# A block-matching convolution kernel on one core: row slots outermost, aggregation and cosine transform copied by ScalarE, transform on 32x32 tiles

## The chip, the cores and the metric

The kernel runs on one core of a Trainium2 chip. The metric is the time of one execution on the device, in microseconds (us); lower is better. Before the change the median of three runs is 6639.3 us (6633.16 to 6649.49).

The core has five engines that run side by side, each through its own list of instructions in order: PE (TensorE, matrix multiplication), DVE (VectorE), ACT (ScalarE), POOL (GpSimd) and SP (SyncE). SP and POOL mostly issue DMAs here. Instructions wait for each other through semaphores.

## The reference

The input x is [8, 32, 128, 128] in float32. Two layers are computed; each normalises its input, computes a branch and adds it to its input. Cut to what matters:

```python
def _L0_conv_ref(x, dct_w, w1, w2, w3, w4, w5, w6, inv_dct_w, agg_w):
    B, C, K, H, W = (8, 32, 8, 128, 128)
    CK = C * K
    # for each pixel: the K of 25 offsets with the lowest 3x3 patch distance,
    # then the K shifted copies of x: [B, C*K, H, W], channel c*K + k
    xb = _patch_match_stack(x)
    dct = _conv(xb, dct_w, groups=C)
    h = jax.nn.relu(_conv(_conv(xb, w1), w2, groups=CK, pad=1))
    h = jax.nn.relu(_conv(_conv(h, w3), w4, groups=CK, pad=1))
    wiener = jax.nn.sigmoid(_conv(_conv(h, w5), w6, groups=CK, pad=1))
    filt = _conv(wiener * dct, inv_dct_w, groups=C)
    return _conv(filt, agg_w)

# --- layer 0 ---
x = x + _L0_conv_ref(_gn(x), ...)
# --- layer 1: one 5x5 kernel on every channel ---
x = x + _L1_conv_ref(_gn(x), L1_conv_kernel, 1, 2)
```

w1, w3, w5 are 256x256 pointwise weights; w2, w4, w6 are 3x3 depthwise weights. The cosine transform (dct) mixes only the 8 copies of one channel: 32 blocks of 8x8.

## The kernel before

**Steps and turns.** An image has 128 rows. The main loop (from L1054) makes 17 steps of 8 rows per image, 136 in all; the last step of an image (n == NS) only finishes rows. Each step has four turns, `i` = 3, 2, 1, 0. In turns 3, 2 and 1 the step does one of the three convolution pairs (pointwise, then depthwise, then its function) for an earlier and earlier stage of the pipeline: conv `i` works on the rows of step s - (i - 1). Turn 0 is the end: cosine transform, product with the result of conv 3, and, a turn later, the aggregation.

**A convolution pair.** The 256 channels are in two halves. The first half goes through `pointwise_t` (PE, L694), a copy by ACT into the buffer `t` (L701), and `depthwise_t`, which does the 3x3 taps as matmuls on PE (pw, L750) and evacuates them by ACT (L763). The second half goes through `pointwise_v` (pv, L670), an ACT copy into `tv` (L678), and `depthwise_v`: first tap on ACT (L721), eight taps on DVE (L724), function on ACT (L728). `t` holds, for each of 128 partitions (4 rows of a group x 32 channels), 4 channel blocks q x 4 row slots x 128 columns. The slots hold the rows that the next matmuls need; SP fills slots from others by DMA, from one half of the partitions to the other (L648, L706, L708).

**Gathering.** Every turn also gathers pixels of a later step: `gather_load` (POOL DMAs, `ib` and `xt`), `gather_select` (ACT, L616 and L617, two 128x1024 operations, twice a turn), `gather_pixels` (PE pg, L631, and an ACT copy into `xb`, L638). After the last copy of a step, POOL stores `xb` to DRAM as `xbd` (L640), one DMA of 1 MB; the layout in DRAM has partition and half as its first two axes.

**The end of a step.** `final_load` (POOL) reads the rows of x (`xr`, L780) and of the gathered copies (`xf`, L790, eight DMAs) for the step before; there is one `xf` buffer. `final_dct` multiplies with the block-diagonal `ldct`, on tiles of 64 rows by 64 columns: 8 matmuls into four `pc` buffers (L809), and DVE multiplies conv 3's result by each of them, straight from PSUM (L817). `final_add` is a generator whose parts run at calls of `next(later)`: the aggregation matmuls `pa` (L830), then, after a `yield`, DVE adds `pa` to `xr` (L838), takes statistics (L839), and POOL stores `xr` as `x1d` (L843).

**PSUM.** `ps_x` has five buffers that go round, for pv, p, pg, pc, pa and others; `ps_dw` has two for pw.

**Order.** PE, DVE and ACT execute in the order in which the code is written (`manual_schedule`); POOL's and SP's order is chosen by the scheduler. POOL's DMAs go through eight semaphores in turn, so an issue waits for the DMA that used the same one before. Work for later images (`prep`, `squares`, `costs`, `places`) and layer 1 of finished ones (`layer1`, `middle`) lies in four queues: "D" for DVE work with a cost in us, which `tick` hands out at a set amount per turn, 40% of a step's in turn 0 and 20% in each other; "A", "P" and "Q" for what follows on ACT and PE.

The turn's order is, shortened (L1065 to L1110):

```python
pointwise_v(i, ...); new_v, new_t = depthwise_v(...), depthwise_t(...)
next(later, None)           # pa on PE, in turn 3
run("P")
if live and not i: final_dct(...)
run("Q"); gather_select(u + 1, (0,)); gather_load(u + 3); tick(b, i)
next(later, None)           # sum on DVE, in turn 3
next(new_v, None)           # eight taps on DVE
pointwise_t(i, ...)
next(kept, None); gather_pixels(u)
next(dt, None)              # pw matmuls of the turn before
run("A"); next(dv, None)    # function of the turn before
gather_select(u + 1, (1,)); next(dt, None)
```

**Set-up.** `mixes` loads `dct_w` into `dq` by 32 small DMAs on SP (L308) and forms `ldct` from it on DVE (L311, L318).

Of the kernel before, what the change touches and what calls it, by code (L numbers as in the profile page):

```python
# [16 lines left out]
P = 128  # L17
C, K, H, W = 32, 8, 128, 128
CK = C * K
# [25 lines left out]
def bm3d_conv_preact(  # L45
# [61 lines left out]
    ldct = const.tile([P, 2, 64], F32, name="ldct")  # L107
# [192 lines left out]
    def mixes():  # L300

        dq = work.tile([P, 2, K], F32, name="dq", tag="dq", bufs=1)
        src = dct_w.rearrange("(m h c i) k a b -> m h k c (i a b)", m=2, h=2, i=K)
        for k in range(K):
            for m in range(2):
                for h in range(2):
                    p = 64 * h + 32 * (k % 2) + 8 * (k // 2)
                    nc.sync.dma_start(dq[p : p + 8, m], src[m, (h + m + 1) % 2, k])  # L308
        m8 = work.tile([P, 8], F32, name="m8", tag="m16", bufs=1)
        yield "D", 1.0, 10  # L310
        nc.vector.tensor_reduce(  # L311
            m8,
            cst[:, C_M32 : C_M32 + C].rearrange("p (a c) -> p c a", c=8),
# [3 lines left out]
        for m in range(2):  # L317
            nc.vector.tensor_tensor(  # L318
                ldct[:, m].rearrange("p (c i) -> p c i", i=K),
                m8.unsqueeze(2).to_broadcast([P, 8, K]),  # L320
                dq[:, m].unsqueeze(1).to_broadcast([P, 8, K]),
                ALU.mult,
            )
# [296 lines left out]
    def gather_pixels(b, s4, f):  # L620
# [18 lines left out]
        if h == 1 and f == 1:  # L639
            nc.gpsimd.dma_start(xbd[b][:, :, R * n : R * (n + 1)], xb)  # L640
# [3 lines left out]
    def rows_before_t(i, b, n):  # L644

        t = tb[i - 1]
        if n < NS:
            nc.sync.dma_start(t[0:64, :, 0], t[64:P, :, 3])  # L648
        else:
            nc.gpsimd.memset(t[0:64, :, 0], 0.0)  # L650
# [29 lines left out]
    def pointwise_t(i, b, n, lhsT, src):  # L680
# [3 lines left out]
        if n == NS and i == 1:  # L684
            nc.gpsimd.memset(t[:, :, 2], 0.0)
        else:
            for q in range(2):
                ps = ps_x.tile([P, 2, 2, W], F32, name=f"p{i}_{b}_{n}_{q}", tag="x")
                for e in range(2):
# [12 lines left out]
                    t[: C * nr, 2 * q : 2 * q + 2, 2 : 2 + nb], ps[: C * nr, :, :nb]  # L702
                )
            for r in range(i - 1) if n == 0 else range(i - 1, 4) if n == NS else ():
                nc.gpsimd.memset(t[C * r : C * (r + 1), :, 2], 0.0)
        nc.sync.dma_start(t[64:P, :, 0:nb], t[0:64, :, 2 : 2 + nb])  # L706
        if nb == 2:
            nc.sync.dma_start(t[0:64, :, 1], t[64:P, :, 2])  # L708
# [23 lines left out]
    def depthwise_t(i, b, n):  # L732
        t = tb[i - 1].rearrange("p q (h k) w -> p q h k w", k=2)
# [35 lines left out]
    def final_load(b, n):  # L769
# [15 lines left out]
        src = xbd[b].rearrange("(j m h c) g y x -> g m h j c y x", j=4, m=2, h=2)  # L785
        for m in range(2):
            for h in range(2):
                for g in range(2):
                    p = 64 * h + C * g
                    nc.gpsimd.dma_start(  # L790
                        xf[p : p + C, m, j0:j1], src[g, m, (h + m + 1) % 2, :, :, ya:yz]
                    )
        return xr, xf, j0, j1

    def final_dct(b, n, acc, xf, j0, j1):

        for r0 in range(0, R, 4):
            a, z = max(r0, j0), min(r0 + 4, j1)
            if a >= z:
                continue  # L800


            pc = [
                ps_x.tile([P, 4, W], F32, name=f"pc_{b}_{n}_{m}_{r0}", tag="x") for m in range(2)
            ]
            for h in range(2):
                for m in range(2):
                    o = 64 * ((h + m + 1) % 2)
                    nc.tensor.matmul(  # L809
                        pc[m][o : o + 64, : z - a],  # L810
                        ldct[64 * h : 64 * h + 64, m],
                        xf[64 * h : 64 * h + 64, m, a:z],
                        start=True,
                        stop=True,
                    )
            for m in range(2):
# [360 lines left out]
```

## Time and profile before

| | |
|---|---|
| median of three runs | 6639.3 us (6633.16 to 6649.49) |
| profiled execution, its own time | 6645.45 us |
| its span | 6643.7 us |
| mean granted PE clock over the span | 0.978 |
| L724, eight taps on DVE, busy | 4032.3 us |
| L750, depthwise matmuls on PE, busy | 2124.6 us |
| L616 and L617, selects on ACT, busy | 1172.1 and 1085.7 us |
| L790, issues of the xf loads on POOL, busy | 651.9 us |
| chain of waits, by engine | PE 43%, DVE 29%, DMA 9%, ACT 8%, POOL 6% |

The span is the time that the profiler saw between the first and the last instruction; the execution's time holds a little more. Busy times of one engine add up to its share of the span; those of different engines overlap. A row of a group reads: line, engine, operation, output <- inputs, shape, count | busy us, mean ns of one | us idle just before, and what ended that idle time. PE's matmuls are pipelined: several run at once, so the mean of one is longer than the busy time divided by the count.

### The profile page before, as it was taken

What the parts mean: (1) busy time and instruction counts of PE and PEld (TensorE: products, weight loads), DVE (VectorE), ACT (ScalarE), POOL (GpSimd) and SP (SyncE); (2) the same over time, 40 slices, a digit from 0 to 9 for tenths busy, and PEclk for the clock granted to TensorE, in tenths of its full rate; (3) what the DMA queues carried; (4) which work ended last, traced back from release to release, by engine and by line L of the source; (5) the groups of instructions that cost most, each with busy time, mean ns of one, the idle gap of its engine ahead of it and who ended that gap; (6) DMA issues with size and microseconds to landing.
All of it is one profiled execution on the core that took longest, in us unless ns stands there. A gap on an engine that the chain in (4) does not pass through costs nothing.

```text
span 6643.7 us, 234197 instructions
## 1 busy us (share of the span) xinstructions
PE 6238.3 (94%) x102306; PEld 3236.5 (49%) x102306; DVE 5862.9 (88%) x8828; ACT 5054.4 (76%) x6698; POOL 3079.3 (46%) x5015
## 2 busy tenths in 40 slices
PE   5898899999999999999999999999999999999997
PEld 1444455544555545544555544554445544454553
DVE  7889988999889998898989998899888999887786
ACT  5787778777787777877778877887769777687772
POOL 8354346444464343643446444464435543344334
PEclk8899999999999999999999999999999999999998
DMA  4555555656555564655646656465555655556553
GB/s 85 126 138 130 131 131 130 148 134 140 131 143 136 130 147 118 149 134 133 144 121 147 147 126 149 120 154 136 130 137 132 148 136 130 125 141 145 137 133 82
DMA packets 770751, 886.20 MB, mean 133 GB/s; under 512 B 248880, under 2 KB 614000, under 8 KB 769728
## 3 DMA queue, kind: packets, MB, share of 16 engines
q0 software_dynamic: 383648, 611.87, 36.9%
q1 hardware_dynamic: 383568, 258.11, 17.6%
q8 instruction: 805, 13.19, 0.9%
q10 hardware_dynamic: 2512, 1.25, 0.1%
q14 instruction: 218, 1.79, 0.1%
HBM read 420.60 MB, written 216.49 MB: 96 GB/s over the span
## 4 chain that ended last, share of the span: by engine, by line
PE 43%; DVE 29%; DMA 9%; ACT 8%; POOL 6%; issue 4%; SPq 0%; ACTq 0%; DVEq 0%; POOLq 0%
DVE acc L724 20%; PE pw L750 14%; PE pv L670 11%; PE p L694 9%; PE pg L631 3%; DMA t<-t 3%; POOL xtd L424 2%; DVE df L444 2%; DVE idx L537 2%; PE pc L809 2%; ACT sel L616 2%; ACT df L452 2%; DMA xf<-xbd 2%; DVE acc L817 1%; PE p L923 1%
## 5 line engine op out<-in xcount | busy, mean ns | idle before, releaser
L724 DVE SCALAR_TENSOR_TENSOR acc<-tv,dwv,acc 128x1024 f32<-128x1024 f32 (+3 forms) x3264 | 4032.3, 1237 | 240.8 <-ACT acc L721 136.8
L750 PE MATMUL pw<-t,dwd 96*32 96x254 f32 (+7 forms) x31680 | 2124.6, 420 | 51.0 <-DMA t<-t 38.4
L750 PEld LDWEIGHTS pw<-t,dwd 96*32 96x32 f32 (+1 forms) x31680 | 1088.4, 110 | 874.5 <-issue 411.2
L616 ACT ACTIVATE sel<-ib,nplace 128x1024 f32<-128x1024 uint8 x1024 | 1172.1, 1145 | 37.4 <-DMA ib<-idxd 37.4
L617 ACT ACTIVATE sel<-sel 128x1024 f32<-128x1024 f32 x1024 | 1085.7, 1060 | 32.5
L694 PE MATMUL p<-acc,lw 128*32 128x256 f32 x16768 | 1002.9, 383 | 24.7 <-ACT tv L678 23.3
L670 PE MATMUL pv<-acc,lw 128*32 128x512 f32 x8448 | 956.2, 590 | 48.7 <-DVE acc L817 43.4
L602 POOL DMA_DIRECT2D ib<-idxd x512 | 292.5, 571 | 1241.8 <-ACT sel L616 1176.2
L790 POOL DMA_DIRECT2D xf<-xbd x1088 | 651.9, 631 | 316.1 <-PE pc L809 180.1
L694 PEld LDWEIGHTS p<-acc,lw 128*32 128x32 f32 x16768 | 579.2, 111 | 437.1 <-issue 79.4
L452 ACT ACTIVATE df<-df 128x786 f32<-128x786 f32 (+2 forms) x576 | 468.6, 861 | 340.5 <-DVE df L444 337.8
L631 PE MATMUL pg<-sel,xt 120*32 120x88 f32 (+1 forms) x24576 | 616.1, 244 | 63.6 <-ACT sel L617 50.7
L631 PEld LDWEIGHTS pg<-sel,xt 120*32 120x32 f32 x24576 | 556.8, 110 | 235.0 <-ACT sel L617 70.1
L678 ACT COPY tv<-pv 128x512 f32<-128x512 f32 (+2 forms) x784 | 437.1, 579 | 305.0 <-PE pv L670 293.0
L444 DVE TENSOR_TENSOR df<-xn 128x786 f32<-128x786 f32 (+2 forms) x576 | 531.6, 973 | 81.2 <-PE pd L459 80.2
L728 ACT ACTIVATE acc<-acc 128x1024 f32<-128x1024 f32 (+3 forms) x408 | 417.3, 1023 | 241.6 <-DVE acc L724 241.3
L763 ACT ACTIVATE acc<-pw 128x512 f32<-128x512 f32 (+2 forms) x808 | 438.5, 573 | 182.7 <-PE pw L750 182.0
L670 PEld LDWEIGHTS pv<-acc,lw 128*32 128x32 f32 x8448 | 286.0, 111 | 534.1 <-issue 428.7
L701 ACT COPY t<-p 128x512 f32<-128x512 f32 x800 | 424.4, 571 | 118.0 <-PE p L694 118.0
L721 ACT ACTIVATE acc<-tv,dwv 128x1024 f32<-128x1024 f32 (+3 forms) x408 | 454.9, 1115 | 33.9 <-PE pa L830 20.6
L670 PE MATMUL pv<-xb,lw 128*32 128x512 f32 x4096 | 473.5, 596 | 0.0
L694 PE MATMUL p<-xb,lw 128*32 128x256 f32 x8192 | 468.5, 379 | 1.0 <-DVE xy L935 0.9
(155 smaller groups left out, 5932.9 us busy)
## 6 DMA issues: line engine op xcount, KB each, us to landing
ib<-idxd POOLq DMA_DIRECT2D x512, 256.0 KB, 4.1
xbd<-xb POOLq DMA_DIRECT2D x128, 1024.0 KB, 5.9
xf<-xbd POOLq DMA_DIRECT2D x960, 128.0 KB, 7.1
t<-t SPq DMA_DIRECT2D x792, 128.0 KB
t<-t SPq DMA_DIRECT2D x384, 256.0 KB
tv<-tv SPq DMA_DIRECT2D x384, 130.0 KB
xt<-xtd POOLq DMA_DIRECT2D x240, 180.0 KB, 3.7
xtd<-xl POOLq DMA_DIRECT2D x192, 96.0 KB, 3.5
```

The source lines that it names most:

```text
L444: nc.vector.tensor_sub(df[:, :, ca:cz], xn[:, r0 : r0 + SR, ca:cz], xn[:, r0 + dy : r0 + dy + SR, ca + dx : cz + dx],)
L452: nc.scalar.activation(df[:, :, ca:cz], df[:, :, ca:cz], AF.Square)
L616: nc.scalar.activation(sel, ib, AF.Square, bias=nplace)
L617: nc.scalar.activation(sel, sel, AF.Relu, scale=-1.0, bias=1.0)
L631: nc.tensor.matmul(pg[C * j : C * (j + 1), :, :, xa:xz], xt[: 8 * QW, f * (NT // 2) + t], sels[j // 2][: 8 * QW, j % 2 * 2 : j % 2 * 2 + 2 ...
L670: nc.tensor.matmul(ps[C * j : C * (j + 1), :hr], lhsT[:, g, P + C * j : P + C * (j + 1)], src(g)[:, h : h + hr], start=g == 0, stop=g == 1,)
L694: nc.tensor.matmul(ps[C * r : C * (r + 1), e, :nb], lhsT[:, g, s], rows[:, r : r + 4 * nb - 3 : 4], start=g == 0, stop=g == 1,)
L721: nc.scalar.activation(acc, rows, AF.Copy, scale=tap)
L724: nc.vector.scalar_tensor_tensor(acc, rows, tap, acc, op0=ALU.mult, op1=ALU.add)
L750: nc.tensor.matmul(pt[u][C * j : C * (j + 1), ka:kz, :nb, xa:xz], dwd[0:hi, i - 1, u, j, dx + 1], t[0:hi, j, ka:kz, :nb, xa + dx : xz + dx ...
L763: nc.scalar.activation(rows[:, u : u + 2 * nh[u] - 1 : 2, :nb], pt[u][:, : nh[u], :nb], funcs[i - 1])
L790: nc.gpsimd.dma_start(xf[p : p + C, m, j0:j1], src[g, m, (h + m + 1) % 2, :, :, ya:yz])
```

## The change

- `ldct` and `dq` are laid out for 32x32 blocks, four per half; the loads of `dct_w` become 64.
- `xbd` holds the 256 channels in natural order. `xb` is stored twice a step, after each group of four rows, by four DMAs each.
- In `t` the row slot becomes the outermost of the free axes: slot, block, column, for block, slot, column. All users of `t` follow.
- `final_load` becomes a generator: the `xr` loads come first, where they were; the `xf` loads (one or two DMAs for each of four pieces of half m and four rows, the channels turned by 32 x s) are issued two pieces at the end of the next turn 3 and two at the end of turn 2.
- `final_dct` does four matmuls on 32x32 tiles for each piece s, from row block q to column block (q + s) mod 4. ACT copies each result over its input in `xf`; DVE then multiplies conv 3's result by `xf`, two instructions for four.
- `final_add` copies `pa` by ACT into a tile `xs`, and adds it one part later; the loop has one more `next(later)` at the end of a turn.

```diff
-    ldct = const.tile([P, 2, 64], F32, name="ldct")
+    ldct = const.tile([P, 4, C], F32, name="ldct")
...
-        for k in range(K):
-            for m in range(2):
-                for h in range(2):
-                    p = 64 * h + 32 * (k % 2) + 8 * (k // 2)
-                    nc.sync.dma_start(dq[p : p + 8, m], src[m, (h + m + 1) % 2, k])
+        for s in range(4):
+            for q in range(4):
+                for c in range(4):
+                    p = C * q + K * c
+                    nc.sync.dma_start(dq[p : p + K, s], src[s // 2, (q + s) % 4, c])
...
-        if h == 1 and f == 1:
-            nc.gpsimd.dma_start(xbd[b][:, :, R * n : R * (n + 1)], xb)
+        if f == 1:
+            for j in range(4):
+                nc.gpsimd.dma_start(
+                    xbd[b].rearrange("(c j g) y x -> j c g y x", j=4, g=2)[
+                        j, :, :, 4 * s4 : 4 * s4 + 4
+                    ],
+                    xb[C * j : C * (j + 1), :, 4 * h : 4 * h + 4],
+                )
...
-            nc.sync.dma_start(t[0:64, :, 0], t[64:P, :, 3])
+            nc.sync.dma_start(t[0:64, 0], t[64:P, 3])
...
                 nc.scalar.copy(
-                    t[: C * nr, 2 * q : 2 * q + 2, 2 : 2 + nb], ps[: C * nr, :, :nb]
+                    t[: C * nr, 2 : 2 + nb, 2 * q : 2 * q + 2].rearrange("p b e w -> p e b w"),
+                    ps[: C * nr, :, :nb],
                 )
...
-        nc.sync.dma_start(t[64:P, :, 0:nb], t[0:64, :, 2 : 2 + nb])
+        nc.sync.dma_start(t[64:P, 0:nb], t[0:64, 2 : 2 + nb])
         if nb == 2:
-            nc.sync.dma_start(t[0:64, :, 1], t[64:P, :, 2])
+            nc.sync.dma_start(t[0:64, 1], t[64:P, 2])
...
-        t = tb[i - 1].rearrange("p q (h k) w -> p q h k w", k=2)
+        t = tb[i - 1].rearrange("p (h k) q w -> p q h k w", k=2)
...
         xf = xbp.tile([P, 2, R, W], F32, name=f"xf_{b}_{n}", tag="xf", bufs=1)
-        src = xbd[b].rearrange("(j m h c) g y x -> g m h j c y x", j=4, m=2, h=2)
+        src = xbd[b].rearrange("(m p) y x -> m p y x", m=2)
+        yield xr, xf, j0, j1
+        for s in range(4):
+            if s:
+                yield
+            m, r0 = s // 2, s % 2 * 4
+            a, z = max(r0, j0), min(r0 + 4, j1)
+            for pa, pz, at in ((0, P - C * s, C * s), (P - C * s, P, 0)):
+                if a < z and pa < pz:
+                    nc.gpsimd.dma_start(
+                        xf[pa:pz, m, a:z],
+                        src[m, at : at + pz - pa, R * n - 3 + a : R * n - 3 + z],
+                    )
+        yield
...
+        parts = [(s, max(s % 2 * 4, j0), min(s % 2 * 4 + 4, j1)) for s in range(4)]
+        parts = [(s, a, z) for s, a, z in parts if a < z]
+        for s, a, z in parts:
+            m = s // 2
+            pc = ps_x.tile([P, 4, W], F32, name=f"pc_{b}_{n}_{s}", tag="x")
+            for q in range(4):
+                o = C * ((q + s) % 4)
+                nc.tensor.matmul(
+                    pc[o : o + C, : z - a],
+                    ldct[C * q : C * (q + 1), s],
+                    xf[C * q : C * (q + 1), m, a:z],
+                    start=True,
+                    stop=True,
+                )
+            nc.scalar.copy(xf[:, m, a:z], pc[:, : z - a])
         for m in range(2):
...
+            nc.vector.tensor_mul(acc[m][:, j0:j1], acc[m][:, j0:j1], xf[:, m, j0:j1])
...
         yield
-        nc.vector.tensor_add(xr, xr, pa)
+        sums = work.tile([P, 2 * W], F32, name=f"xs_{b}_{n}", tag="xs", bufs=1)
+        sums = sums[:, : nr * nw].rearrange("p (r w) -> p r w", w=nw)
+        nc.scalar.copy(sums, pa)
+        yield
+        nc.vector.tensor_add(xr, xr, sums)
...
                 next(dt, None)
+                next(later, None)
                 kept, dv, dt = dv, new_v, new_t
...
-                    fins[s - 1] = final_load(*steps[s - 1])
+                    loads = final_load(*steps[s - 1])
+                    fins[s - 1] = next(loads)
+                if 0 <= s - (1 if not i else 2) < len(steps):
+                    for _ in range({0: 0, 3: 2, 2: 2, 1: 0}[i]):
+                        next(loads)
```

## The prediction

> **What bounds the kernel now.** I read the busy shares first, then the table of stretches, cut at the starts of the cosine transform (one stretch is one step of the main loop), then the waits, then the groups with their forms, and last the order of time around one transform.
>
> ```profile
> span 6643.7 us, 234197 instructions
> PE 6238.3 (94%) x102306; PEld 3236.5 (49%) x102306; DVE 5862.9 (88%) x8828; ACT 5054.4 (76%) x6698; POOL 3079.3 (46%) x5015
> ```
>
> PE is busy nearly throughout, DVE close behind, ACT has a quarter of its time free. An average hides which of them sets a step:
>
> ```profile
> core 0: us, PE busy (x) PEld busy (x) DVE busy (x) ACT busy (x) POOL busy (x), PEclk, DMA share, GB/s
> 3230.70:3278.60 47.90, 44.29 (x761) 22.17 (x758) 45.01 (x110) 35.20 (x47) 21.55 (x40) 1.00 0.69 163
> 3278.60:3325.70 47.10, 44.90 (x753) 21.84 (x752) 40.81 (x36) 35.36 (x47) 18.86 (x34) 0.96 0.51 124
> 6254.20:6297.00 42.80, 42.80 (x756) 23.08 (x752) 33.99 (x31) 34.97 (x44) 12.03 (x22) 1.00 0.54 135
> ```
>
> The third stretch lies in the last image, where no next image is prepared: DVE has 34 us of work and PE runs without a gap, 42.8 us. In the first two DVE has 41 to 45 us, and both engines stand idle for 2 to 6 us. So PE is the floor, and above it comes what PE and DVE wait for each other.
>
> ```profile
> DVE xr L838 <- PE pa L830: 237.1, 57, 9.9
> PE pv L670 <- DVE acc L817: 43.4, 25, 3.0
> PE pw L750 <- DMA t<-t: 38.4, 27, 4.0
> ```
>
> Columns: us in total, times, longest. One step shows how the first two feed each other (start, us, engine):
>
> ```profile
> 3278.64 2.17 PE L809 MATMUL pc<-xf,ldct 64*64 64x512 f32 x16
> 3289.24 5.34 PE L670 MATMUL pv<-acc,lw 128*32 128x512 f32 x32 [2.20 <-DVE acc L817]
> 3288.51 2.47 DVE L817 TENSOR_TENSOR acc<-acc,pc 128x512 f32<-128x512 f32 x4
> 3295.51 0.42 DVE L838 TENSOR_TENSOR xr<-xr,pa 128x256 f32<-128x256 f32 x1 [4.53 <-PE pa L830]
> 3288.62 1.06 ACT L728 ACTIVATE acc<-acc 128x1024 f32<-128x1024 f32 x1 [6.08 <-DVE acc L724]
> ```
>
> The transform is done by 3281, but DVE reaches its products (L817) only at 3288.5, behind eight taps. Until then they hold four of the five ps_x buffers, so pv waits 2.2 us and then runs 5.34 us where others take 3.6. The aggregation pa comes behind pv, and DVE, which reaches L838 early, waits 4.53 us for it. ACT idles 6 us in the same stretch. These rows price the rest:
>
> ```profile
> L670 PE MATMUL pv<-acc,lw 128*32 128x512 f32 x8192 | 941.6, 598 | 48.7 <-DVE acc L817 43.4 <-ACT t L701 4.6
> L631 PE MATMUL pg<-sel,xt 120*32 120x88 f32 x20480 | 546.9, 246 | 63.6 <-ACT sel L617 50.7 <-DVE acc L817 3.6 <-ACT ct L529 2.8
> L678 ACT COPY tv<-pv 128x512 f32<-128x512 f32 x752 | 426.7, 589 | 301.6 <-PE pv L670 289.6 <-DMA t<-t 5.6 <-DMA tv<-tv 4.5
> L817 DVE TENSOR_TENSOR acc<-acc,pc 128x512 f32<-128x512 f32 x496 | 308.1, 679 | 14.3 <-PE pc L809 14.1
> L809 PE MATMUL pc<-xf,ldct 64*64 64x512 f32 x1984 | 269.5, 611 | 12.1 <-ACT tmp_b L265 7.6 <-DVE acc L817 3.8 <-ACT t L701 0.6
> ```
>
> Busy time over count is the pace: 0.115 us for each pv instruction of 512 columns, 0.027 for pg, 0.136 for pc, so 16 x 0.136 = 2.17 us a transform. 496 / 4 gives 124 whole transforms among the 136 steps.
>
> **The change, part by part.** Sums are against this execution: 6645.45 us, its span and 1.75 around it, 6 us above the median of 6639.3.
>
> *Transform on 32x32 tiles.* A step has 16 matmuls for 8; the trace shows each as two instructions, so 32 of 512 columns for 16. The trace has no 32x32 tile. If four run at a time, as at the 0.115 pace of pv, this takes 32 x 0.115 = 3.68 us: +1.51 x 124 = +187 us. If tiles are limited only by the spacing of instructions, as in pg, 32 x 0.027 = 0.85 us: -1.32 x 124 = -163 us. The nearest rows are those on 64x64: four run at once there although two share each row half and two each column half. The change turns the columns with s, so that the 16 of a step lie on 16 different tiles. If the two instructions of a matmul follow each other on its tile, at 4 x 0.115 = 0.46 each, that is 0.92, and with some stagger I take 1.2: -0.97 x 124 = **-120 us**.
>
> The row against a rule: on 64x64 the two row halves write the same pc buffer, in different partitions, and still four run together (2.17 us for 16 instructions; one after another, each 0.46 us, they would take 7.4). The Trainium skill, "TensorEngine Tiling (Array Packing)", Gotcha 1: PSUM Pressure, says that different row tiles cannot use one PSUM bank at the same time. By it the four row tiles of one s would follow each other, and the sum would have the +187 in place of the -120; the trace shows it not to hold for separate partitions.
>
> *Results copied by ScalarE.* Four copies of 128x512 at 0.589 and one of the sums, 128x256 (between 0.264 for 128x128, L571, and 0.476 for 128x400, L529; I take 0.38): 2.74 x 124 = 340 us of ACT, 76% to 81%. They stand where ACT waits today: for L728's taps 241 us, for pg 156. What is queued behind them is a select pair and xb's copy; their readers come a turn later. With the cover gone, PE's waits on ACT (sel 50.7, tv 23.3, squares 46.6, together 121) could double: 0 to +120, I take **+40**. In return pc is free after ACT's copy: PE's waits on L817 (43.4 + 3.8 + 3.6) go, **-51** (0 to -51).
>
> *DVE.* Four products of 0.679 become two of 128x1024 in SBUF (nearest: L519, 1.225): -0.27 x 124 = -33 us. The sum moves one place on, behind the taps, and no longer waits for pa: up to -237 us of idle. DVE is not the floor, so PE gets only part: it idles 248 us between 340 and 6500 us, of which 51 are counted above. 0 to -100, I take **-30**.
>
> *Row slot outermost.* The same bytes, but a partition's piece is one run of 2 or 4 KB where it was four of 512 B or 1 KB. The number and size of instructions stay; L750 takes 382 ns with split rows and 384 with whole ones, so PE and ACT see no difference. Of PE's 38.4 us for t: **-20** (0 to -38).
>
> *POOL and SP.* The store of xb goes from 128 issues to 1024, of the kind that takes 0.63 (L790): 1024 x 0.63 - 91 = +554; loads from 1088 to 920: -106. POOL rises by about 450 us, to 53%. xf is now overwritten by ACT and read by DVE, so its loads wait for L825 instead of pc, but they are moved two turns on, where the product is long done; POOL's 180 us behind pc go. The loads land a median 6.9 us after issue (16.7 at most), with a turn of at least 10 us to spare. Stores stand before the ib loads in the queue, twice a step, waiting for xb. 0 to +60, I take **+10**.
>
> *Start.* dq is loaded by 64 small DMAs for 32; these 32 held SP for 23 us and ended at 46.3. DVE reads dq at 53.4, in order; the new ones end near 69, land near 71: 17.5 us of DVE, of which 6 were a wait for xl later: **+11** (0 to +18).
>
> Sum: -120 + 40 - 51 - 30 - 20 + 10 + 11 = -160 us. From the median, 6480.
>
> **Rivals.**
> - *Four tiles at a time* (slower). The place is pc's stretch on PE: 3.68 us, +187 for -120, all else as before: 6479 + 307 = 6786. For it: no row shows more than four matmuls together. Against it: two streams per row half on 64x64 already go side by side. It decides once pc takes 2.5 us a step (2.17 + 40 / 124).
> - *ACT takes DVE's place.* ACT's copies need 4 x 0.589 = 2.36 us and PE's next tiles want these buffers: pc costs 2.36 (+24 for -120), the 51 stays: 6479 + 144 + 51 = 6674. For it: ACT is in order, and pc's copies stand behind the pw evacuation. Against it: ACT is idle 4 to 6 us there.
> - *Both engines come free.* With L838's wait gone DVE runs ahead: -163 - 51 - 80 - 20 + 20 = -294: 6345. For it: in steps with 41 to 45 us of DVE work both engines idle. Against: the steps of 42.8 have no gap to win.
>
> **How the numbers follow.** Forecast 0.52, four at a time 0.20, ACT 0.18, both free 0.10. A change below 0.3% can't be told from none (the three runs span 0.25%). Faster is forecast and both-free, 0.62; ACT's case straddles no change, 0.08, and slower, 0.10; with the 0.20, slower is 0.30. The forecast's own range, with its unknowns, is 6400 to 6560. Down to 6360 takes in half of the third rival; up to 6720 all of ACT's and about half of four-at-a-time, whose bound is soft. Left out: some 0.19.
>
> **What would show it.** Right: pc near 1.2 us a step; no wait of pv on the product; no wait of DVE on pa; ACT near 5400 us with the wait for L728's taps cut; steps of the last image at 41.8, not 42.8. Wrong: pc above 2.5 us, or those steps longer than 42.8; PE waits on ACT's copies above 100 us; POOL's waits on landings passing into ib or dsum, and from there to select or the box sums; a gap over 18 us at DVE near 53 us.

## The result and the profile after

The changed kernel takes 6670.1 us (median of eight runs, 6659.7 to 6690.2) where the kernel before takes 6642.0 in the same series: a ratio of 1.004 (95% interval 1.0028 to 1.0053). It is slower by 28 us; 6480 was forecast. Two lines of the page give the span and the busy shares:

```profile
span 6673.2 us, 240476 instructions
...
PE 6209.6 (93%) x104418; PEld 3260.7 (49%) x104418; DVE 5840.5 (88%) x8574; ACT 5333.5 (80%) x7362; POOL 3386.8 (51%) x5743
```

PE has 29 us less to do than before and DVE 22 us less, yet the span is 30 us longer: both wait more. The table of stretches (columns as before) shows where. The steps of an image are counted here from 0; the first row is step 1 of the fourth image, from its second transform to its third, the second a step of the last image:

```profile
2785.48:2843.36 57.88, 52.25 (x832) 23.98 (x838) 51.79 (x88) 40.27 (x54) 27.91 (x46) 0.94 0.54 143
6286.00:6328.30 42.30, 42.30 (x780) 22.68 (x772) 33.73 (x29) 36.76 (x51) 15.21 (x29) 1.00 0.51 139
```

Where PE has no gap, a step is 0.5 to 0.6 us shorter than before (42.8 us there): the new transform is faster. But step 1 takes 57.9 us where the kernel before takes 53.1 in that image, and it is so in each of the second to seventh images: 57.8 to 58.1 us, 52.9 to 55.0 before, 27 us in the six together. The same step of the kernel before:

```profile
2782.66:2835.78 53.12, 50.12 (x812) 26.40 (x808) 51.12 (x90) 42.82 (x56) 21.41 (x32) 1.00 0.57 136
```

The waits, in us in total, times and longest:

```profile
POOL x1d L855 <- DVE xr L850: 554.0, 89, 14.6
DVE acc L731 <- ACT acc L728: 433.5, 130, 15.7
PE pc L816 <- DMA xf<-xbd: 34.2, 6, 6.0
PE pw L757 <- DMA t<-t: 29.0, 15, 3.9
```

Two rows of the kernel before go with them:

```profile
DVE acc L724 <- ACT acc L721: 136.8, 128, 4.7
POOL x1d L843 <- DVE xr L838: 259.7, 68, 14.1
```

DVE no longer waits for `pa` before the sum (237.1 before). Instead its taps wait 433.5 us for their first tap on ACT (L728, formerly L721), where that was 136.8: together 374 us have become 434. POOL waits twice as long for the sum (259.7 before), and PE has a wait that was not there, six times, once in each of those images: for `xf`. PE's wait of `pv` for the products is gone, as forecast. The groups and two places of PE's timeline give the transform:

```profile
L816 PE MATMUL pc<-xf,ldct 32*32 32x512 f32 x3968 | 221.0, 624 | 56.7 <-DMA xf<-xbd 34.2 <-ACT tmp_b L265 12.7 <-ACT xf L823 7.5
```

```profile
2785.36 1.09 PE L816 MATMUL pc<-xf,ldct 32*32 32x512 f32 x16
2792.08 3.88 PE L816 MATMUL pc<-xf,ldct 32*32 32x512 f32 x16 [5.63 <-DMA xf<-xbd]
...
6325.55 1.33 PE L816 MATMUL pc<-xf,ldct 32*32 32x512 f32 x32
```

221.0 / 124 is 1.78 us a transform in place of 2.17; in the gapless steps it is 1.33 to 1.41 where the kernel before shows 1.95:

```profile
6254.29 1.95 PE L809 MATMUL pc<-xf,ldct 64*64 64x512 f32 x16
```

In step 1 the transform stops half-way for 5.63 us. What makes `xf` late stands in POOL's timeline ahead of that place:

```profile
2742.48 24.58 POOL L424 DMA_DIRECT2D xtd<-xl  x30 [0.66 <-DMA xl<-xs]
...
2770.13 2.00 POOL L787 DMA_DIRECT2D xr<-in_x_dram  x4
...
2775.18 2.33 POOL L855 DMA_DIRECT2D x1d<-xr  x4
2777.56 1.61 POOL L801 DMA_DIRECT2D xf<-xbd  x3
2779.16 0.78 POOL L896 DMA_DIRECT2D xy<-x1d  x1
2779.94 0.64 POOL L898 DMA_DIRECT2D xm<-x1d  x1
2780.62 0.76 POOL L901 DMA_DIRECT2D xy<-x1d  x1
...
2789.53 0.52 POOL L801 DMA_DIRECT2D xf<-xbd  x1 [0.32 <-DMA ib<-idxd]
```

POOL issues the 30 stores of `xtd`, prepared data of the next image, in one block of 24.6 us. Everything that belongs to the running step comes behind it, and with it the first loads of layer 1 (`xy`, `xm`). The last piece of `xf` is issued at 2789.5, 4 us after PE has begun the transform, and lands 4.5 us later.

### The profile page after: what moved, and what is told of

Same layout as the page of the kernel before. It is cut to its first block, busy times and chain, and to the rows that moved or that the text cites. A ratio compares the mean times of both kernels' runs of the same rounds, so it can differ in the third digit from the quotient of the medians.

```text
span 6673.2 us, 240476 instructions
## 1 busy us (share of the span) xinstructions
PE 6209.6 (93%) x104418; PEld 3260.7 (49%) x104418; DVE 5840.5 (88%) x8574; ACT 5333.5 (80%) x7362; POOL 3386.8 (51%) x5743
## 4 chain that ended last, share of the span: by engine, by line
PE 42%; DVE 26%; ACT 10%; DMA 9%; POOL 7%; issue 6%; SPq 0%; ACTq 0%; DVEq 0%; POOLq 0%
DVE acc L731 16%; PE pw L757 14%; PE pv L676 10%; PE p L700 9%; PE pg L631 3%; POOL xtd L424 3%; DVE idx L537 2%; ACT sel L616 2%; DVE df L444 2%; DMA t<-t 2%; ACT df L452 2%; DVE acc L825 2%; PE pc L816 2%; DMA out_dram<-xy 2%; PE p L935 1%
## 5 line engine op out<-in xcount | busy, mean ns | idle before, releaser
L731 DVE SCALAR_TENSOR_TENSOR acc<-tv,dwv,acc 128x1024 f32<-128x1024 f32 (+3 forms) x3264 | 4034.1, 1237 | 537.3 <-ACT acc L728 433.5
L757 PEld LDWEIGHTS pw<-t,dwd 128*32 128x32 f32 (+1 forms) x31680 | 1095.8, 111 | 881.8 <-issue 422.0
L700 PE MATMUL p<-acc,lw 128*32 128x256 f32 x16768 | 1005.2, 384 | 24.5 <-ACT tv L684 22.3
L676 PE MATMUL pv<-acc,lw 128*32 128x512 f32 x8448 | 963.1, 591 | 15.3 <-ACT xs L848 13.1
L801 POOL DMA_DIRECT2D xf<-xbd x920 | 497.4, 547 | 377.2 <-DVE acc L825 132.1
L631 PE MATMUL pg<-sel,xt 120*32 120x88 f32 (+1 forms) x24576 | 622.3, 245 | 70.4 <-ACT sel L617 51.2
L641 POOL DMA_DIRECT2D xbd<-xb x1024 | 550.5, 544 | 250.6 <-ACT xb L638 225.9
L855 POOL DMA_DIRECT2D x1d<-xr x544 | 275.2, 512 | 614.9 <-DVE xr L850 554.0
L735 ACT ACTIVATE acc<-acc 128x1024 f32<-128x1024 f32 (+3 forms) x408 | 417.2, 1022 | 180.4 <-DVE acc L731 179.7
L728 ACT ACTIVATE acc<-tv,dwv 128x1024 f32<-128x1024 f32 (+3 forms) x408 | 454.7, 1115 | 31.0 <-PE pa L838 18.5
```

Of the source, the lines that this page charges most:

```text
L631: nc.tensor.matmul(pg[C * j : C * (j + 1), :, :, xa:xz], xt[: 8 * QW, f * (NT // 2) + t], sels[j // 2][: 8 * QW, j % 2 * 2 : j % 2 * 2 + 2 ...
L641: nc.gpsimd.dma_start(xbd[b].rearrange("(c j g) y x -> j c g y x", j=4, g=2)[j, :, :, 4 * s4 : 4 * s4 + 4], xb[C * j : C * (j + 1), :, 4 * ...
L676: nc.tensor.matmul(ps[C * j : C * (j + 1), :hr], lhsT[:, g, P + C * j : P + C * (j + 1)], src(g)[:, h : h + hr], start=g == 0, stop=g == 1,)
L700: nc.tensor.matmul(ps[C * r : C * (r + 1), e, :nb], lhsT[:, g, s], rows[:, r : r + 4 * nb - 3 : 4], start=g == 0, stop=g == 1,)
L728: nc.scalar.activation(acc, rows, AF.Copy, scale=tap)
L731: nc.vector.scalar_tensor_tensor(acc, rows, tap, acc, op0=ALU.mult, op1=ALU.add)
```

## The experiments

Medians and ratios are against runs of the kernel before on the same chip. The runs are spread over five chips, and the intervals are 6 to 10 us to either side, so a difference of some 10 us between two kernels of this list can't be told from none. "Alone" means the kernel before with that part of the change.

### Each part alone

slot_only, the row slot outermost in `t` and nothing else:

```diff
-        t = tb[i - 1].rearrange("p q (h k) w -> p q h k w", k=2)
+        t = tb[i - 1].rearrange("p (h k) q w -> p q h k w", k=2)
```

> The kernel before with the row slot outermost in t and nothing else. My theory (the loss of the whole change comes from late loads of xf and from ACT's extra work, not from here): PE's wait for t falls from 38 to about 25 us, the time goes down by 10 to 20 us, ratio 0.997 to 0.999. Rival (the new strides make ACT's copies L701 or PE's reads of t slower): those groups' mean times rise and the ratio is 1.002 or more.

Measured: 6623.9 us, 0.998 (0.9971 to 0.9988). PE's wait for `t` fell from 38.4 to 21.0 us. The part gains 17 us.

agg_only, the aggregation copied by ACT and added behind the taps:

```diff
-        nc.vector.tensor_add(xr, xr, pa)
+        sums = work.tile([P, 2 * W], F32, name=f"xs_{b}_{n}", tag="xs", bufs=1)
...
+        nc.scalar.copy(sums, pa)
+        yield
+        nc.vector.tensor_add(xr, xr, sums)
...
+                next(later, None)
                 kept, dv, dt = dv, new_v, new_t
```

> The kernel before with the aggregation copied by ACT and added behind the taps, and nothing else. My theory: DVE's wait on pa (237 us) does not go, it turns up before the first tap on DVE as a wait on ACT's L721, which waits for pa too, because conv 3's accumulator has one buffer; POOL's wait on the sum rises from 260 to above 500 us; ratio 1.000 to 1.004. Rival (the forecast's step: the wait goes and DVE runs ahead): DVE's waits on pa and on L721 together fall by 150 us or more, ratio 0.99 to 0.996.

Measured: 6709.5 us, 1.0106 (1.0093 to 1.0119), a loss of 69 us. Its waits:

```profile
POOL x1d L847 <- DVE xr L842: 556.4, 92, 17.0
DVE acc L724 <- ACT acc L721: 464.4, 129, 11.0
PE pw L750 <- DMA t<-t: 55.9, 33, 4.4
```

The wait moved to the first tap, as the theory said, but its price was far too small. The step that grew most is again step 1 of an image (3.6 us in the mean of six images); steps 7 and 2 follow with 1.9 and 1.4.

dct_only, the transform on 32x32 tiles with ACT's copies, the new layout of `xbd` and its 1024 stores, and the later loads of `xf`:

```diff
+            pc = ps_x.tile([P, 4, W], F32, name=f"pc_{b}_{n}_{s}", tag="x")
+            for q in range(4):
+                o = C * ((q + s) % 4)
...
+            nc.scalar.copy(xf[:, m, a:z], pc[:, : z - a])
```

> The kernel before with the transform on 32x32 tiles, its copies by ACT, the new layout of xbd and the later loads of xf, but with the old t and the old aggregation. My theory: this part holds the loss: in one step of each image pc waits for xf 5 us or more (34 us in all), the short steps at an image's end are some 3 us longer for ACT's copies, and the gapless steps of the last image are 0.6 us shorter; ratio 1.002 to 1.006. Rival (the loss lies with the aggregation): ratio 0.995 to 1.000.

Measured: 6627.8 us, 0.9982 (0.9973 to 0.9991). The first theory, that this part holds the loss, fell: it gains 13 us, and PE waits for `xf` 7.4 us in the whole run, at most 2.2 at a time.

after_early, the changed kernel with all pieces of `xf` loaded at the end of turn 0:

```diff
-                    for _ in range({0: 0, 3: 2, 2: 2, 1: 0}[i]):
+                    for _ in range({0: 4, 3: 0, 2: 0, 1: 0}[i]):
```

> The changed kernel with all four pieces of xf asked for at the end of turn 0, where the kernel before asks for them, for turns 3 and 2. My theory (late loads make some 30 us of the loss): PE's wait of pc for xf (34 us, 6 times) goes, the step after an image's first is 5 us shorter, 6635 to 6650 us, ratio to before 0.999 to 1.002. Rival (the loads' place does not matter, the loss is ACT's work): the wait goes but the time stays at 6665 to 6675.

Measured: 6661.9 us, 1.0029 (1.0019 to 1.0038), between the two. PE's wait for `xf` is gone, but its wait for `t`, 29.0 us in the changed kernel, is 56.2 here, and step 1 still takes 54.4 to 58.8 us. Taken away in this manner, the wait brings only 8 us.

Two parts gain 30 us together and the third loses 69. So the questions are why the later sum costs, and why the transform gains so little.

### What of the later sum costs

agg_dummy: ACT's copy alone, into a tile that nothing reads; DVE still adds from PSUM in the old place:

```diff
+        sums = work.tile([P, 2 * W], F32, name=f"xs_{b}_{n}", tag="xs", bufs=1)
+        sums = sums[:, : nr * nw].rearrange("p (r w) -> p r w", w=nw)
+        nc.scalar.copy(sums, pa)
         nc.vector.tensor_add(xr, xr, pa)
```

> The kernel before, plus one ScalarE copy of the 32 aggregated channels a step into a tile that nothing reads; VectorE still adds from PSUM, in the old place. Only the ScalarE time of the copy is added (136 times some 0.35 us, 48 us of ScalarE). Theory 'the place of the sum costs': 0.998 to 1.002 of the time before (6630 to 6655 us), because ScalarE has idle time. Rival 'the copy costs': 1.006 to 1.011 (6680 to 6715), most of what the whole aggregation part cost.

Measured: 6861.9 us, 1.0338 (1.0322 to 1.0354), above both theories. The copy wasn't alone: the second reader of a PSUM tile is made to wait for the first,

```profile
DVE xr L841 <- ACT xs L840: 632.9, 111, 13.1
```

and ACT reaches the copy only behind the work that stands before it in its list. The run doesn't answer its question. It shows what waiting for ACT's copy in the old place costs, 222 us; a sum that reads the copy can pay, if at all, only in a later place.

agg_late: the sum behind the taps, straight from PSUM:

```diff
         yield
+        yield
         nc.vector.tensor_add(xr, xr, pa)
...
+                next(later, None)
                 kept, dv, dt = dv, new_v, new_t
```

> The kernel before, with the sum and its statistics moved behind the eight taps, but read straight from PSUM with no ScalarE copy. Theory 'the place of the sum costs': before its taps VectorE waits in any case, for pv, its evacuation and ScalarE's first tap; sum and statistics (0.42 + 0.43 us) stood in that wait for nothing and now come on top, 0.85 x some 128 steps = 109 us of VectorE, and the store of the sum is later by the taps: 1.006 to 1.012 (6680 to 6720). Wait of the taps on ScalarE's first tap 430 to 480 us in place of 137. Rival 'the copy costs': 0.997 to 1.002.

Measured: 6762.2 us, 1.0184 (1.0169 to 1.0199), above the theory's range, and the taps wait 522 us for the first tap: the place of the sum costs, and more without the copy than with it. Here `pa` holds one of the five PSUM buffers through eight taps (PE waits 19.6 us for the sum itself); whether that makes the whole difference is not shown. The copy is not what costs; the kernel with it is 53 us faster.

agg_store: agg_only, with the stores of `x1d` issued half a turn later:

```diff
         nc.vector.bn_stats(stats[b][:, n], xr)
+        yield
+        yield
         for j in range(4):
```

> The aggregation part alone (copied by ScalarE and added behind the taps), but the stores of the sums issued half a turn of the main loop later on GpSimd's queue, behind the next load of indices, so that GpSimd no longer stands waiting for the sum. Theory 'GpSimd's queue behind the sum costs': 1.000 to 1.004 of the time before, GpSimd's wait for the sum falls from 556 us to under 200, and the late loads (ib, t, xf) go. Rival 'VectorE's order costs': 1.008 to 1.012, as without this edit, although the wait falls.

Measured: 6746.6 us, 1.016 (1.0145 to 1.0175). POOL's wait for the sum stayed at 547.7 us: the store moved behind the next load of indices, and POOL reached it early all the same. What the run was to take away it didn't take away, so it says nothing on the queue except that moving the store cost another 37 us.

agg_last: agg_only, except that the last step of an image adds in the old place. after_last: the same edit in the changed kernel:

```diff
+        if n == NS:
+            nc.vector.tensor_add(xr, xr, pa)
+        else:
+            sums = work.tile([P, 2 * W], F32, name=f"xs_{b}_{n}", tag="xs", bufs=1)
...
+            nc.scalar.copy(sums, pa)
+            yield
+            nc.vector.tensor_add(xr, xr, sums)
```

> The aggregation part alone (copied by ScalarE, added behind the taps), except in the last step of each image, where VectorE adds from PSUM in the old place. Theory 'the last sum': the second layer of an image begins when its last sum is made; made later, the second layer's first loads of xy and xm fall on GpSimd's queue behind the 30 stores of xtd instead of ahead of them, and on the sync queue one transfer of t of each image falls behind one of tv. So the steps 1 and 2 of the images after the first, which took 5.0 us more than before, lose all or most of this: 6665 to 6685 us, 1.004 to 1.007. Rival 'every step pays': only one sum in 17 is moved back, 6700 to 6712, 1.009 to 1.011.

> The changed kernel, except that in the last step of each image VectorE adds from PSUM in the old place. Theory 'the last sum': xy and xm are loaded ahead of the xtd stores again, PE's wait for xf in step 1 (5.6 us in the changed kernel) goes: 6630 to 6650 us, 0.998 to 1.001. Rival 'every step pays': 6660 to 6675, 1.003 to 1.005.

Measured: 6687.3 us, 1.0061 (1.0047 to 1.0075), 22 us less than agg_only and 2 us above the range; and 6639.5 us, 1.000 (0.9991 to 1.001), 31 us less than the changed kernel and inside it. With one sum in 17 moved back the changed kernel is as fast as the kernel before. POOL's timeline of after_last at the same place:

```profile
2707.33 0.76 POOL L904 DMA_DIRECT2D xy<-x1d  x1
...
2737.54 23.71 POOL L424 DMA_DIRECT2D xtd<-xl  x29 [0.91 <-issue]
...
2767.11 1.21 POOL L858 DMA_DIRECT2D x1d<-xr  x2
...
2777.57 0.52 POOL L801 DMA_DIRECT2D xf<-xbd  x1 [0.68 <-DMA ib<-idxd]
```

Layer 1 of an image is handed out when its last sum is made. Made in the old place, its first loads go out ahead of the block of `xtd`. The last `xf` is issued at 2777.6; the transform begins at 2779.0. That is not quite early enough, for PE still waits here, but shorter:

```profile
2781.62 2.56 PE L816 MATMUL pc<-xf,ldct 32*32 32x512 f32 x16 [1.51 <-DMA xf<-xbd]
```

In the whole run PE waits 10.0 us for `xf`, in 8 places, where the changed kernel waits 34.2. Step 1 is 23.5 us shorter in the six images together, so most of the 31 us lie there.

before_fill: the kernel before, with two more statistics behind the taps:

```diff
+        yield
+        fill = work.tile([P, 2, 6], F32, name=f"fill_{b}_{n}", tag="fill")
+        for k in range(2):
+            nc.vector.bn_stats(fill[:, k], cst[:, 0:256])
```

> The kernel before, its sum and store in the old place; behind the taps VectorE takes two more statistics of 256 elements of a constant into a tile that nothing reads, about 0.85 us a step, what sum and statistics take. No store and no load is later by itself. Theory 'VectorE's time on the path': what remains of the loss (some 35 us) is VectorE work that stood in a wait for nothing and now is on the path: 1.004 to 1.010, 6667 to 6707. Rival 'the stores are late, not VectorE': 0.998 to 1.002.

Measured: 6677.2 us, 1.0052 (1.0038 to 1.0066), 36 us more, in the theory's range. It is the size of what is left: after_last to the kernel without the later sum, next, is 35 us. The agreement in size is the evidence; that kernel adds VectorE work, where the changed one moves it.

after_noagg: the changed kernel with the aggregation as it was:

```diff
-        nc.scalar.copy(sums, pa)
-        yield
-        nc.vector.tensor_add(xr, xr, sums)
+        nc.vector.tensor_add(xr, xr, pa)
...
-                next(later, None)
```

> The changed kernel with the aggregation as it was: row slot and 32x32 transform only. If the parts add up (row slot 0.998, transform 0.998): 0.995 to 0.997, 6605 to 6620 us, faster than both kernels. If the parts disturb each other: 0.998 to 1.001.

Measured: 6604.7 us, 0.995 (0.9935 to 0.9965), faster than both kernels. Its waits beside those above:

```profile
DVE xr L846 <- PE pa L838: 224.6, 61, 9.0
DVE acc L731 <- ACT acc L728: 143.4, 127, 4.7
```

DVE idles here 368 us at these two places and 434 in the changed kernel. Sum and statistics (0.42 and 0.43 us) stand between them: ACT makes its first tap while DVE makes the sum. Behind the taps they fill no wait.

### Why the transform gains so little

noagg_direct: after_noagg without ACT's copies of the transform:

```diff
-            nc.scalar.copy(xf[:, m, a:z], pc[:, : z - a])
-        for m in range(2):
-            nc.vector.tensor_mul(acc[m][:, j0:j1], acc[m][:, j0:j1], xf[:, m, j0:j1])
+            nc.vector.tensor_mul(acc[m][:, a:z], acc[m][:, a:z], pc[:, : z - a])
```

> The changed kernel with the aggregation as it was and without the ScalarE copies of the transform: VectorE multiplies straight from PSUM, four products of 128x512 a step. Beside the run without that edit (6605 us): the prediction's terms say that the copies cost 40 us of ScalarE and save 51 of PE's waits for products and some 20 of VectorE, so without them 6615 to 6650. Rival 'the copies cost more than they save': 6570 to 6600.

Measured: 6605.9 us, 0.9947 (0.9934 to 0.9961), the same as with the copies; both expectations missed. ACT has 250 us less to do and PE again waits for the products:

```profile
PE pv L676 <- DVE acc L823: 56.3, 27, 3.2
```

The copies remove that wait and bring no time.

before_half: the kernel before with the transform of the second half of the channels left out:

```diff
-                    for m in range(2):
...
+                    pc[o : o + 64, : z - a],
+                    ldct[64 * h : 64 * h + 64, 0],
+                    xf[64 * h : 64 * h + 64, 0, a:z],
```

> The kernel before with half of the transform left out: the second half of the channels is not transformed, and both products read the first half's result. 8 PE instructions a step in place of 16, some 1.09 us a step less, 124 x 1.09 = 135 us of PE; VectorE, ScalarE, loads and stores unchanged; two PSUM buffers fewer are held a step. Theory 'PE's time there is covered outside the gapless steps' (VectorE and the waits set the other steps): 0.990 to 0.997, 6575 to 6620 us; the steps of 42.8 us fall to some 41.7, the mean of the others by less than 0.4. Rival 'PE is the floor throughout', which the prediction took: 0.977 to 0.983, 6490 to 6525.

Measured: 6623.6 us, 0.9972 (0.9962 to 0.9983). PE's timeline shows that it was no test of either: half the instructions, the same time, and the gapless steps stayed at 42.8 us.

```profile
6234.71 1.93 PE L806 MATMUL pc<-xf,ldct 64*64 64x512 f32 x8
```

The instructions left out were those of two of the four tiles. What the 16 us come from, two PSUM buffers fewer or the order in the queues, is open.

before_rows: half of the transform left out in the other direction; the products of rows 4 to 7 read the result of rows 0 to 3. All four tiles are in use, and buffers and products are those of before_half, its control:

```diff
+            if pc is None or not whole:
+                pc = [
+                    ps_x.tile([P, 4, W], F32, name=f"pc_{b}_{n}_{m}_{r0}", tag="x") for m in range(2)
+                ]
```

> The kernel before with half of the transform left out: only the first four rows of a step are transformed, and the products of the other four read the same result. 8 PE instructions on all four tiles in place of 16, so some 0.97 us of PE less in 112 whole steps, 109 us; PSUM buffers and products as in the run that left out half the channels (6624 us), which saved no PE time. Theory 'PE's time is covered outside the gapless steps': 10 to 40 us below that run, 6584 to 6614; gapless steps 41.8. Rival 'PE is the floor throughout': 80 to 110 below it, 6514 to 6544.

Measured: 6600.7 us, 0.9945 (0.993 to 0.9961), in the theory's range.

```profile
6208.01 1.09 PE L809 MATMUL pc<-xf,ldct 64*64 64x512 f32 x8
```

Now the transform takes 1.09 us for 1.95, and the gapless steps 41.9. That is 0.86 us in 120 whole steps, 103 us of PE; against before_half 23 us of time came of it, about a fifth (by the intervals of the two ratios 18 us, give or take 13). It is a mean of two kinds of step. In the gapless ones the whole 0.86 us come back; besides six steps of the last image, step 12 of every image is one of them:

```profile
1708.79:1748.74 39.95, 39.95 (x613) 19.41 (x609) 31.63 (x29) 17.56 (x25) 9.75 (x18) 1.00 0.46 119
```

This is the kernel before; in before_rows the step takes 39.08. These 14 steps make some 12 of the 23 us, and the other 106 share the rest: PE is not the floor throughout.

before_stores: the kernel before with each store of `xb` cut into eight:

```diff
-        if h == 1 and f == 1:
-            nc.gpsimd.dma_start(xbd[b][:, :, R * n : R * (n + 1)], xb)
+        if f == 1:
+            for j in range(4):
+                nc.gpsimd.dma_start(
+                    xbd[b][C * j : C * (j + 1), :, 4 * s4 : 4 * s4 + 4],
+                    xb[C * j : C * (j + 1), :, 4 * h : 4 * h + 4],
+                )
```

> The kernel before with each store of xb cut into eight by channels and rows, as the changed kernel issues them: 1024 stores in place of 128, the same bytes to the same places, some 460 us more of GpSimd. Theory 'the stores take the gain back': 1.003 to 1.010, 6660 to 6705 us. Rival 'GpSimd has the room', which the prediction took at +10 us: 0.999 to 1.002.

Measured: 6696.9 us, 1.0083 (1.0069 to 1.0097), 57 us more. Most of them lie in steps 1 and 2 (5.6 and 2.7 us in the median of six images); in step 1 PE stops in the middle of the transform, once in each of six images, not for `xf` but for the products:

```profile
PE pc L813 <- DVE acc L821: 47.2, 6, 7.9
```

noagg_half_stores: after_noagg with `xb` stored once for eight rows, 512 stores; noagg_sync_stores: these on SP's queue; after_sync: the latter in the whole changed kernel:

```diff
-        if f == 1:
+        if h == 1 and f == 1:
             for j in range(4):
-                nc.gpsimd.dma_start(
+                nc.sync.dma_start(
                     xbd[b].rearrange("(c j g) y x -> j c g y x", j=4, g=2)[
-                        j, :, :, 4 * s4 : 4 * s4 + 4
+                        j, :, :, R * n : R * (n + 1)
                     ],
-                    xb[C * j : C * (j + 1), :, 4 * h : 4 * h + 4],
+                    xb[C * j : C * (j + 1)],
                 )
```

> The changed kernel with the aggregation as it was (6605 us), and xb stored once for eight rows, in 4 pieces, instead of twice for four rows: 512 stores in place of 1024, the same bytes. Theory 'the stores take the gain back': some half of the 56 us that 896 more stores cost in the kernel before, 6570 to 6585. Rival 'their number is no matter here': 6600 to 6612.

> As the run with 512 stores, but these are issued on the sync queue, between the transfers of t and tv, so that GpSimd issues fewer than in the kernel before. Theory 'GpSimd's queue': 6545 to 6575, below the run with 512 stores on GpSimd. Rival 'the sync queue is no better': a store there waits for xb and holds the t transfers behind it, PE's wait for t rises above 60 us: 6600 to 6650.

> The changed kernel whole, with xb stored once for eight rows in 4 pieces on the sync queue: the last sum of an image stays late, GpSimd's queue is relieved by 1024 stores. Theory 'GpSimd's queue around the xtd stores makes xf late': PE's wait for xf (34 us) falls below 5 and the time to 6620 to 6645 us, 0.997 to 1.001. Rival 'the late start of the second layer costs by itself': 6655 to 6675, although the wait for xf goes.

Measured: 6646.5 us, 1.0001 (0.9991 to 1.0012), 42 us worse with half the stores, outside both expectations; 6592.7 us, 0.9924 (0.9912 to 0.9937), the fastest kernel of all, 12 us below after_noagg, where the theory wanted 30 or more and the rival 6600 us or more; and 6642.2 us, 1.000 (0.999 to 1.0009), 28 us below the changed kernel and in the theory's range. In the first, step 1 is 4.4 us longer than in after_noagg in the mean of six images, and PE waits for `xf` again, 33.0 us for 9.1:

```profile
PE pc L814 <- DMA xf<-xbd: 33.0, 6, 7.1
```

So in these kernels it is not the number of stores that costs; the time goes with PE's wait for `xf`. With the stores off POOL's queue that wait is 0.5 us in noagg_sync_stores, and in after_sync 6.1 us, a little above the 5 of the theory, although layer 1 still starts late. But after_sync does not settle how much the late start costs by itself: moving the stores brings 12 us without the later sum too, and between these two kernels the later sum still costs 49 us.

## Why the prediction was wrong

**DVE, "the sum moves one place on ... and no longer waits for pa" (-30, bounds 0 to -100): the step that failed first.** The wait at L838 did go, but it came back at the next instruction, where the first tap was late as well: 374 us of idle became 434. The two waits had one cause, PE and ACT reaching this place later than DVE, and the sum stood between them for nothing. The row to look at was DVE's wait on L721, 136.8 us in 128 times, right behind L838. Instead of -30 the part brings 31 + 35 us, 65 before rounding: 35 fit DVE's 0.85 us a step behind the taps (before_fill, which adds that time there and moves no sum and no store, loses 36), 31 are the last sum of an image. This split is not exact: with the stores on SP's queue the later sum, the last one included, costs 49 us with little wait for `xf`.

**POOL, "with a turn of at least 10 us to spare" (+10): failed in one step of 17.** The time to spare was taken from the landing of the loads, not from their place in a queue whose order the scheduler chooses and which holds a block of 25 us once an image. In the changed kernel the last piece of `xf` is issued 4 us after the transform begins; with the last sum in the old place 1.4 us ahead of it. Most of the 31 us lie here: two cures that work in different ways, after_last and after_sync, cut PE's wait from 34.2 us to 10.0 and 6.1 and bring 31 and 28 us, some 12 of the 28 by the move of the stores alone. The wait for `xf` is not all of it: after_early removes it and brings 8, because PE then waits for `t`. Which share belongs to `xf` and which to the other loads behind the block stays open. That a sum made later also starts layer 1 later is missing from the prediction altogether; it priced the queue by what was added to it and not by what moved within it. The added time itself came out smaller than forecast, POOL's busy time rose by 307 us and not by 450.

**The transform (-120): the mechanism right, the worth wrong.** Tiles do run beside each other, more than four at a time: 1.33 us for 32 instructions undisturbed, near the 1.2 assumed, so 0.62 us a step and not 0.97, since the undisturbed figure before is 1.95 and not the mean of 2.17. But the sum took PE's time for the kernel's time in every step. The profile said otherwise: of the three stretches shown, only the one in the last image had no gap. before_rows puts the exchange at about a fifth; 0.62 x 124 x 0.22 is 17 us. The part alone measured 13, but it also carries ACT's copies, 896 more stores and the later loads, so the agreement may be chance. The Trainium skill, "TensorEngine Tiling (Array Packing)", Gotcha 1: PSUM Pressure, has different row tiles unable to share a PSUM bank; here four row tiles write one `pc` buffer in different partitions, and the 1.33 us are well below the 3.68 that the prediction worked out for four tiles at a time.

**ACT's copies (+40) and the waits on L817 (-51).** Both in sign and kind as said: `pv` no longer waits for the products, ACT is busy 5333 us for 5400 forecast. Net, noagg_direct gives zero where the terms gave -11. ACT's wait for the taps (L735) was cut only from 241 to 180, and PE's waits on ACT did not double (selects 51.2 us, squares 37.7 and 12.5, `tv` 22.3 and 14.3; new are 13.1 for the copy of `pa` and 7.5 for those of the transform).

**Row slot (-20): right**, -17 alone. **Start (+11):** the first transform begins 2.5 us later, and DVE has no gap near 53 us; the wait for `dq` did not come.

**The rivals.** Four tiles at a time is refuted by the 1.33 us. Both engines free did not come. "ACT takes DVE's place" gave 6674 and lies next to the measured time, but not by its mechanism: without ACT's copies the time is the same. The loss has a cause that none of the three named.

What stays open: whether a second buffer for conv 3's result, which `pa` reads and the first tap overwrites, would let DVE's taps start before `pa` and make the later sum pay; this wasn't tried. Nor is it settled why PE waits for the products in before_stores, only in which step.

## What to carry to other kernels

Before counting a wait as won, look at what the next instruction on that engine waits for; if it is the same late producer, the work between the two waits was free and becomes dear when moved. A stretch without gaps prices engine time only for stretches like it, so find all of them; elsewhere ask what a microsecond of that engine is worth, by an experiment that takes away half of the work on all tiles. Where a scheduler orders the DMA queues, an edit of some other engine's order moves loads past each other; check the place of the densest block in the queue, for that is where a small shift shows in every image.

## What the runs showed of the hardware

On 64x64 tiles, 16 instructions on four tiles take 1.95 us, 8 on two tiles 1.93, 8 on four tiles 1.09; on 32x32 tiles, 32 on sixteen take 1.33 to 1.41. Divided by the instructions on each tile that is 0.49, 0.48, 0.55 and 0.67 to 0.71 us for one of 512 columns. So in these rows the count of instructions per tile sets the time far more than the number of tiles, and leaving out the work of whole tiles saved none.

In step 1 of the changed kernel the granted clock is 0.94 in the mean, where the same step of the kernel before has 0.97 to 1.00. Cut more finely, around the stop at 2786 (columns as before):

```profile
2785.36:2790.20 4.84, 1.09 (x20) 0.18 (x16) 4.73 (x4) 3.25 (x6) 2.23 (x5) 1.00 0.96 287
2790.20:2797.00 6.80, 4.92 (x24) 1.17 (x28) 4.41 (x5) 1.57 (x3) 3.63 (x7) 0.50 0.69 187
2797.00:2843.36 46.36, 46.36 (x796) 22.76 (x797) 42.77 (x81) 35.57 (x46) 22.18 (x34) 1.00 0.47 122
```

While PE stands, the granted clock falls to 0.50, and it stays there for 6.8 us. The 16 transform instructions that follow the stop take 3.88 us, the 16 ahead of it 1.09; one of them lasts 1.03 to 1.06 us, ahead of the stop 0.59 to 0.61. The pieces of `xf`, which land one by one, are the other part: in after_last, where the clock is 1.00 through the shorter stop of 1.51 us, each instruction lasts 0.58 to 0.61 us, and the 16 still take 2.56. The depthwise matmuls at full clock right after take 5.35 us as ever. So the stop costs some 8 us at that place, more than its length; step 1 as a whole is 4 to 5 us longer.
